# Moving the gated fusion of a GNN block from VectorE to ScalarE and GpSimd

## The chip, the cores and the metric

The kernel runs on one core of a Trainium2 chip. A core has five engines that run their own instruction streams in order[...]: PE (TensorE, matrix products and transposes), DVE (VectorE), ACT (ScalarE), POOL (GpSimd) and SP (SyncE, which only issues transfers here). POOL issues transfers as well. PEld in a profile is the weight load of TensorE. The metric is the device time of one execution in microseconds (us). The time before is the median of three runs, 2973.59 us (2967.89 to 2974.53).

## What is computed

Four graph layers run one after another on x (4096 x 256) with one 0/1 matrix adj (4096 x 4096). Each layer normalizes x, takes the positive part as h and adds its result to x. Layers 1 to 3 (a mean over neighbours, a graph attention, a dense masked attention) are not touched. The change lies in layer 0, which combines an attention branch with a gated state-space branch:

```python
Wh = h @ W
...
h_attn = attn @ Wh
h_enh = jax.nn.silu(_ln(Wh @ fe1_w + fe1_b, fe_ln_g, fe_ln_b)) @ fe2_w + fe2_b
...
hs = (h_part * jax.nn.silu(z) + h_part * D) @ out_w + out_b
c_proj = C @ cp_w + cp_b
hs = hs * (1.0 + c_proj)
comb = jnp.concatenate([h_attn, hs], axis=1)
g = jax.nn.sigmoid(jax.nn.silu(_ln(comb @ g1_w + g1_b, g_ln_g, g_ln_b)) @ g2_w + g2_b)
fused = g * h_attn + (1.0 - g) * hs + h_enh
return _ln(fused, ln_g, ln_b)
```

The kernel writes the sigmoid as (tanh(t/2) + 1)/2, and the fusion as g * (h_attn - hs) + (hs + h_enh).

## The kernel before

**Stages.** The attention of layer 0 runs to about 600 us of the profiled execution. After it comes the dense part of layer 0, to about 1200 us, then the neighbour mean of layer 1 (to about 1470 us), the attention of layer 2 and the dense attention of layer 3. Only the dense part is concerned.

**Tiling.** The 4096 rows are 32 tiles of 128 rows. The dense part takes them in NB = 8 blocks of BT = 4 tiles, so an elementwise instruction over a block of 256 features is 128 partitions x 1024 f32. `dense(b)` is a generator with 31 stretches between its yields. `run_staggered(..., 16)` starts a new block every 16 ticks, so the second half of block b is written down beside the first half of block b + 1. Blocks are called b0 to b7 here.

**What sets the order.** The stagger gives the order in which the program is written. The compiler's scheduler then settles an order for each engine, and each engine keeps it: an instruction whose input is late holds up everything behind it on the same engine.

**The steps around the change**, by line of the profile:

- L906 (DVE, x4) evacuates the gate's product from PSUM and adds the bias, into `f`, which is the block's slice of `xs` (the profile shows it as xs).
- L910 (ACT) is tanh(f/2). L911 (DVE) is (f + 1) * dh. L912 (DVE) is f * 0.5 + hs, where hs already holds hs + h_enh. dh and that sum were made by POOL at L887 and L888.
- `normed(f, "ol")`: DVE takes statistics (L123 and L124, tiles ol_st and ol_mv), L114 adds eps, POOL takes the power -1/2 (L117, ol_rs), DVE forms the offset (L750, ol_off), and ACT scales the four tiles (L753).
- L915 and L916 (POOL) multiply by the weight and add x. `measure` then takes statistics of the new x (L123 again, pl_st) for layer 1.

Beside these run steps of the next block: L857 (DVE, x4) evacuates the products of the state branch into sz, L866 (DVE, x4) those of henh, L873 (DVE, x4) those of hs. All of these matmuls (PE, L155) write into a PSUM pool `psm` of four buffers with one tag, so the fourth hs product needs the buffer that the fourth L866 frees. After hs come the transposes (L737) for the fifth matmul stage.

**A shared buffer.** `dh` of block b and `obc` of block b + 1 use one SBUF buffer:

```python
obc = d.tile([P, BT, D], F32, tag="obc", name="obc")
...
dh = d.tile([P, BT, D], F32, tag="obc", name="dh")
```

POOL writes the next obc (L815) only when the last reader of dh, L911, is done.

**Counting beside it.** The degree counts of layer 1 are taken in the same stretch. POOL issues loads of adj (L174) into four buffers, and ACT runs two Sign instructions with an accumulator on each (L181). 18 tiles of 4 quarters are counted here: 144 Sign instructions, the last of them at about 868 us. A load is issued when the Sign instructions have released its buffer.

Of the kernel before, what the change touches and what calls it, by code (L numbers as in the profile page):

```python
# [11 lines left out]
F32 = mybir.dt.float32  # L12
# [3 lines left out]
AF = mybir.ActivationFunctionType  # L16
ALU = mybir.AluOpType
# [4 lines left out]
P = 128  # L22
# [19 lines left out]
def kernel(ctx: ExitStack, tc: tile.TileContext, w: dict, out: bass.AP):  # L42
    nc = tc.nc
# [5 lines left out]
    NB = NT // BT  # L49
# [416 lines left out]
    with ExitStack() as l0:  # L466
# [10 lines left out]
        with ExitStack() as es:  # L477
# [158 lines left out]
            with ExitStack() as ps_:  # L636
                wp = ps_.enter_context(tc.tile_pool(name="l0_w0", bufs=1))
                work = ps_.enter_context(tc.tile_pool(name="l0_prep", bufs=2))
                small = ps_.enter_context(tc.tile_pool(name="l0_ps", bufs=4))
# [60 lines left out]
        with ExitStack() as es:  # L700
# [4 lines left out]
            small = es.enter_context(tc.tile_pool(name="l0_s", bufs=4))  # L705
# [68 lines left out]
            def dense(b):  # L774
# [94 lines left out]
                hs = d.tile([P, BT, D], F32, tag="hs", name="hs")  # L869
# [16 lines left out]
                dh = d.tile([P, BT, D], F32, tag="obc", name="dh")  # L886
# [15 lines left out]
                f = ha  # L902
# [5 lines left out]
                        yield  # L908

                nc.scalar.activation(f, f, AF.Tanh, scale=0.5)  # L910
                nc.vector.scalar_tensor_tensor(f, f, 1.0, dh, ALU.add, ALU.mult)  # L911
                nc.vector.scalar_tensor_tensor(f, f, 0.5, hs, ALU.mult, ALU.add)  # L912
                yield
                yield from normed(f, "ol")
                nc.gpsimd.tensor_tensor(f, f, wide(ln_g), ALU.mult)  # L915
# [3 lines left out]
                else:  # L919
                    for k in range(1, EARLY):  # L920
                        early(k)

            w1, early1 = [], []

            def early(b):

                if not w1:
                    w1.append(code_p.tile([P, KD, D], F32, tag="a", name="w1", bufs=AHEAD))
                    nc.gpsimd.dma_start(
                        out=w1[0], in_=w["L1_gnn_WT"].rearrange("(k p) m -> p k m", p=P)  # L930
                    )
                h = d.tile([P, BT, 2 * S + 1], F32, tag="bc", name="h")[:, :, 0:D]
                hT = d.tile([P, KD, BW], F32, tag="whT", name="hT", bufs=2)
                for _ in halves1(b, h, hT, w1[0], pst, psm, early1[0][:, b, :, :, :]):
                    pass

            def with_counts(b):
                n = COUNTED * NQ // NB
                for k, _ in enumerate(dense(b)):
                    if k < n:  # L940
                        tally.count(b * n + k)
                    yield
# [58 lines left out]
    with ExitStack() as es:  # L1001
# [10 lines left out]
        small = es.enter_context(tc.tile_pool(name="l1_s", bufs=4))  # L1012
# [155 lines left out]
    with ExitStack() as l3:  # L1168
# [4 lines left out]
        with ExitStack() as es:  # L1173
            wp = es.enter_context(tc.tile_pool(name="l3_w", bufs=1))
            work = es.enter_context(tc.tile_pool(name="l3_prep", bufs=2))
            small = es.enter_context(tc.tile_pool(name="l3_ps", bufs=4))
# [54 lines left out]
        small = l3.enter_context(tc.tile_pool(name="l3_small", bufs=4))  # L1231
# [165 lines left out]
```

## Time and profile before

| what | value |
|---|---|
| median of three runs | 2973.59 us |
| profiled execution, own time | 2971.09 us |
| its span | 2969.1 us |
| PE busy over the span | 2862.3 us, 96% |
| DVE, ACT, POOL busy | 1904.9, 1260.4, 960.9 us |
| L910 tanh, x8 | median 1056 ns |
| L911, x8 | 1215 to 1226 ns |
| L912, x8 | 1224 to 3007 ns, median 2478 |
| L915, POOL, x8 | 2346 to 2362 ns |
| L887, POOL, x8 | 2354 to 2382 ns |
| L815 obc, POOL, x8 | 1893 to 1912 ns |
| start of L910 in b0 to b7 | 701.92, 776.07, 850.73, 918.88, 988.08, 1057.26, 1126.43, 1179.62 us |
| 630 to 870 us: PE, DVE, ACT, POOL busy | 227.07, 116.45, 223.20, 116.57 of 240 us |
| 870 to 1150 us: the same | 275.20, 147.37, 88.35, 108.16 of 280 us |

The last two rows divide the dense part: as long as the Sign instructions run, ACT is busy for 93% of the time; after that ACT is busy for a third and PE for 98%. A busy share says which engine has little room, not which wait ends last; the chain of waits in each stretch says that.

### The profile page before, as it was taken

The page shows a single profiled execution, that of the slowest core. Times are in us where ns is not written, and L with a number is a line of the kernel's source. Part 1 is how long each engine was busy: PE and PEld are TensorE (multiplying, and loading weights), DVE is VectorE, ACT ScalarE, POOL GpSimd, SP SyncE. Part 2 cuts the span into 40 slices and gives each one's busy share as a digit, 9 for nine tenths or more (in the row PEclk, how much of TensorE's full clock was granted, in tenths as well). Part 3 has the DMA queues.
Part 4 walks back from the last instruction along what each step waited for, and adds up shares of the span by engine and source line. Part 5 has one row for each costly group of instructions (what it writes and reads, how often), then busy time and mean ns, then how long its engine had stood idle before and what let it go on. Part 6 is the DMA issues. An engine that isn't in the chain of part 4 may idle for free.

```text
span 2969.1 us, 35221 instructions
## 1 busy us (share of the span) xinstructions
PE 2862.3 (96%) x13381; PEld 2336.3 (79%) x13381; DVE 1904.9 (64%) x3491; ACT 1260.4 (42%) x1922; POOL 960.9 (32%) x725
## 2 busy tenths in 40 slices
PE   7999999999999999899999998999999999999999
PEld 6888888856556666788788777888888888888888
DVE  6877767345555554577688888656765666566553
ACT  6765555389963333994354333343111112111111
POOL 6576665545543333321055555540000000000000
PEclk9999999999999999999999999999999999999999
DMA  6966654154520001796432212002111111111100
GB/s 168 224 140 136 137 127 127 44 86 78 78 47 8 8 8 22 192 243 193 144 120 79 78 65 78 29 20 82 36 62 36 38 39 58 39 34 62 34 8 8
DMA packets 109177, 238.62 MB, mean 80 GB/s; under 512 B 10752, under 2 KB 31216, under 8 KB 100304
## 3 DMA queue, kind: packets, MB, share of 16 engines
q1 hardware_dynamic: 68512, 159.34, 15.4%
q0 software_dynamic: 37696, 69.11, 15.0%
q10 hardware_dynamic: 2800, 7.92, 0.8%
q8 instruction: 105, 1.72, 0.2%
q14 instruction: 64, 0.52, 0.1%
HBM read 265.63 MB, written 37.81 MB: 102 GB/s over the span
## 4 chain that ended last, share of the span: by engine, by line
PE 67%; DVE 8%; ACT 7%; POOL 6%; issue 6%; DMA 5%; POOLq 0%; SPq 0%; DVEq 0%; ACTq 0%
PE acc L408 16%; PE acc L1329 15%; PE s L155 15%; PE mm L155 10%; PE acc L1060 8%; POOL y L359 4%; ACT sign L181 3%; DVE run L292 3%; DVE y L355 2%; DMA turned<-codesT 2%; DMA ab_row<-l_ab_d 1%; PE q_ps L155 1%; PE tp L737 1%; DMA a<-in_adj_dram 1%; DMA l_ab_d<-abT_sb 1%
## 5 line engine op out<-in xcount | busy, mean ns | idle before, releaser
L408 PE MATMUL acc<-v,y 128*128 128x257 f32 x4096 | 929.7, 386 | 13.0 <-ACT hp L971 6.3
L408 PEld LDWEIGHTS acc<-v,y 128*128 128x128 f32 x4096 | 777.9, 192 | 126.9 <-ACT hp L971 8.0
L359 POOL TENSOR_TENSOR y<-y,turned 128x1024 f32<-128x1024 f32 (+1 forms) x272 | 549.0, 2039 | 324.8 <-DVE y L355 228.8
L387 ACT ACTIVATE y<-y,sdst 128x512 f32<-128x512 f32 (+1 forms) x544 | 350.3, 689 | 421.2 <-POOL y L359 421.1
L1329 PE MATMUL acc<-v,y 128*128 128x257 f32 x2048 | 454.5, 380 | 0.4 <-DVE rden L1337 0.4
L155 PE MATMUL s<-qT,hT 128*128 128x256 f32 x2048 | 445.2, 379 | 0.7 <-ACT qT L1277 0.7
L1322 ACT ACTIVATE y<-y 128x1024 f32<-128x1024 f32 x128 | 132.2, 1055 | 714.3 <-DVE y L1321 710.0
L155 PEld LDWEIGHTS s<-qT,hT 128*128 128x128 f32 x2048 | 389.0, 190 | 54.2 <-ACT qT L1277 1.4
L1329 PEld LDWEIGHTS acc<-v,y 128*128 128x128 f32 x2048 | 387.1, 190 | 55.9 <-issue 0.8
L355 DVE SCALAR_TENSOR_TENSOR y<-ab_row,cdst,b 128x512 f32<-128x512 f32 (+1 forms) x544 | 366.3, 709 | 64.1 <-PE acc L408 55.9
L181 ACT ACTIVATE sign<-a,limits 128x1024 bf16<-128x1024 bf16 x256 | 293.9, 1148 | 20.7 <-DMA a<-in_adj_dram 15.2
L1291 DVE SCALAR_TENSOR_TENSOR y<-code,s 128x512 f32<-128x512 bf16 x256 | 175.8, 688 | 101.0 <-PE s L155 100.7
L292 DVE SCALAR_TENSOR_TENSOR run<-turned,v,run 128x512 f32<-128x512 bf16 (+1 forms) x270 | 186.5, 691 | 59.9 <-ACT turned L536 56.4
L292 DVE SCALAR_TENSOR_TENSOR run<-turned,dst,run 128x512 f32<-128x512 bf16 x240 | 180.4, 752 | 33.7 <-DMA turned<-codesT 30.1
L1321 DVE TENSOR_TENSOR y<-y,top 128x1024 f32<-128x1024 f32 x128 | 146.2, 1213 | 43.0 <-PE top L1315 43.0
L1298 DVE TENSOR_TENSOR mx<-mx,y 128x512 f32<-128x512 f32 x224 | 154.8, 691 | 7.4
L536 ACT ACTIVATE turned<-cT,log_wide 128x1024 bf16<-128x1024 bf16 x128 | 139.1, 1104 | 41.0 <-PE cT L531 32.1
L174 POOL DMA_DIRECT2D a<-in_adj_dram x128 | 76.5, 599 | 216.1 <-ACT sign L181 161.4
L155 PE MATMUL mm<-kept 128*128 128x512 f32 x288 | 136.8, 615 | 3.3 <-ACT sz L848 2.2
L1060 PE MATMUL acc<-early,eq 128*128 128x512 f32 x512 | 129.0, 401 | 6.9 <-DVE early L457 5.3
L1060 PE MATMUL acc<-late,eq 128*128 128x512 f32 x512 | 122.8, 391 | 0.0
L1060 PEld LDWEIGHTS acc<-early,eq 128*128 128x128 f32 x512 | 96.3, 190 | 30.3 <-DVE early L457 5.5
(236 smaller groups left out, 3013.1 us busy)
## 6 DMA issues: line engine op xcount, KB each, us to landing
turned<-codesT SPq DMA_DIRECT2D x36, 1024.0 KB, 4.8
adj_t<-in_adj_dram POOLq DMA_DIRECT2D x128, 256.0 KB, 5.5
codesT<-turned SPq DMA_DIRECT2D x32, 1024.0 KB, 5.5
a<-in_adj_dram POOLq DMA_DIRECT2D x128, 256.0 KB, 4.8
code<-codesT SPq DMA_DIRECT2D x128, 256.0 KB, 5.8
code<-codesT SPq DMA_DIRECT2D x64, 512.0 KB, 7.2
ab_row<-l_ab_d ACTq DMA_DIRECT2D x14, 512.0 KB, 4.7
xt<-in_x_dram SPq DMA_DIRECT2D x8, 512.0 KB, 3.8
```

Source lines behind the costliest of these rows:

```text
L155: nc.tensor.matmul(out=ps, lhsT=lhsT_of(k), rhs=rhs_of(k), start=(k == 0), stop=(k == n - 1))
L181: nc.scalar.activation(sign, self.came[g], AF.Sign, bias=limits[:, v : v + 1], accum_out=over[:, t, v, q : q + 1],)
L292: nc.vector.scalar_tensor_tensor(to, code, dst, st["run"], ALU.subtract, ALU.min)
L355: nc.vector.scalar_tensor_tensor(y[:, :, k, :], st["ab"][:, 0, :, :], self.cdst[:, c + k : c + k + 1], st["b"], ALU.add, ALU.max,)
L359: nc.gpsimd.tensor_tensor(y, y, mask[:, :, c % QT : c % QT + 2, :], ALU.subtract)
L387: nc.scalar.activation(y[:, :, k, :], y[:, :, k, :], AF.Exp, bias=self.sdst[:, c + k : c + k + 1],)
L408: nc.tensor.matmul(out=accs[b][r], lhsT=y1[:, r, j % 2, :], rhs=self.v[:, j, 0 : D + 1], start=(j == 0), stop=(j == NT - 1),)
L1060: nc.tensor.matmul(out=acc, lhsT=eqs[c // (NT // 2)][:, ts(c % (NT // 2), P)], rhs=v1[c // BT][:, c % BT, :, :], start=(c == 0), stop=(c = ...
L1291: nc.vector.scalar_tensor_tensor(y[:, :, c : c + 2, :], st["code"][:, :, c : c + 2, :], -BIG / UNIT, ps, ALU.mult, ALU.add,)
L1298: nc.vector.tensor_tensor(mx, mx, y[:, :, c : c + 2, :], ALU.max)
L1321: nc.vector.tensor_tensor(part, part, top, ALU.subtract)
L1329: nc.tensor.matmul(out=accs[r], lhsT=st["y"][:, r, c, :], rhs=v3[:, c, :], start=(c == 0), stop=(c == NT - 1),)
```

## The change

In all blocks but the last, the two VectorE instructions become one ScalarE and two GpSimd instructions. A column of 0.5 is made once as the bias.

```diff
                 nc.scalar.activation(f, f, AF.Tanh, scale=0.5)
-                nc.vector.scalar_tensor_tensor(f, f, 1.0, dh, ALU.add, ALU.mult)
-                nc.vector.scalar_tensor_tensor(f, f, 0.5, hs, ALU.mult, ALU.add)
+                if b < NB - 1:
+
+                    nc.scalar.activation(f, f, AF.Identity, scale=0.5, bias=half)
+                    nc.gpsimd.tensor_tensor(f, f, dh, ALU.mult)
+                    nc.gpsimd.tensor_tensor(f, f, hs, ALU.add)
+                else:
+                    nc.vector.scalar_tensor_tensor(f, f, 1.0, dh, ALU.add, ALU.mult)
+                    nc.vector.scalar_tensor_tensor(f, f, 0.5, hs, ALU.mult, ALU.add)
                 yield
...
+            half = small.tile([P, 1], F32, name="half", bufs=1)
+            nc.gpsimd.memset(half, 0.5)
             w1, early1 = [], []
```

ScalarE forms 0.5 * tanh + 0.5, GpSimd multiplies by dh and adds hs. In the changed file these are L913, L914 and L915; the old L911, L912, L915 and L916 become L917, L918, L921 and L922. The dh buffer is now read last by GpSimd's own multiplication, so the next obc waits for that instead of for VectorE.

## The prediction

> **What bounds the kernel now.** I first looked at the windows of busy time, because the page's 96% for PE is a mean over stages. In the dense part there are two regimes: ACT busy 223.20 of 240 us from 630 to 870 us, PE busy 275.20 of 280 us from 870 to 1150 us. Then I asked who waits for whom on PE in the dense part (us in total, times, longest):
>
> ```profile
> PE mm L155 <- DVE henh L866: 7.9, 6, 1.9
> PE tp L737 <- ACT t L753: 6.4, 12, 2.2
> PE tp L737 <- DVE whT L741: 0.8, 1, 0.8
> ```
>
> PE loses little, and its largest loss is to the evacuation of henh, behind the changed instructions on DVE. The timeline of b4 (start, duration, engine, line; brackets: idle time before and what ended it) shows where it comes from:
>
> ```profile
> 988.08 1.06 ACT L910 ACTIVATE xs<-xs 128x1024 f32<-128x1024 f32 x1 [3.23 <-DVE xs L906]
> 989.16 1.23 DVE L911 SCALAR_TENSOR_TENSOR xs<-xs,dh 128x1024 f32<-128x1024 f32 x1 [1.12 <-ACT xs L910]
> 990.30 0.74 DVE L857 SCALAR_TENSOR_TENSOR sz<-mm,c_b_hz,sz 128x512 f32<-128x512 f32 x1
> 990.47 1.90 POOL L815 TENSOR_TENSOR obc<-kept,gain 128x1024 f32<-128x1024 f32 x1 [3.96 <-DVE xs L911]
> 990.97 2.48 DVE L912 SCALAR_TENSOR_TENSOR xs<-xs,hs 128x1024 f32<-128x1024 f32 x1
> ...
> 994.69 0.74 DVE L123 BATCH_NORM_STATS2 ol_st<-xs 128x6 f32<-128x256 f32 x2
> ...
> 997.43 1.04 POOL L117 TENSOR_TENSOR ol_rs<-ol_ve,mhalf 128x4 f32<-128x4 f32 x1 [5.07 <-DVE ol_ve L114]
> 998.50 0.16 DVE L750 SCALAR_TENSOR_TENSOR ol_off<-ol_mv,ol_rs 128x4 f32<-128x4 f32 x1 [0.83 <-POOL ol_rs L117]
> ...
> 998.70 2.08 ACT L753 ACTIVATE xs<-xs,ol_off,ol_rs 128x256 f32<-128x256 f32 x4 [9.57 <-DVE ol_off L750]
> ...
> 1000.86 2.35 POOL L915 TENSOR_TENSOR xs<-xs,kept 128x1024 f32<-128x1024 f32 x1 [2.38 <-ACT xs L753]
> 1001.19 5.34 PE L155 MATMUL mm<-kept,sz 128*128 128x256 f32 x24
> 1003.28 2.35 POOL L916 TENSOR_TENSOR xs<-xs,xt 128x1024 f32<-128x1024 f32 x1
> ...
> 1005.67 0.75 DVE L123 BATCH_NORM_STATS2 pl_st<-xs 128x6 f32<-128x256 f32 x2 [5.58 <-POOL xs L916]
> ...
> 1007.20 0.39 DVE L866 TENSOR_TENSOR henh<-mm,kept 128x256 f32<-128x256 f32 x1
> ...
> 1007.65 1.99 PE L155 MATMUL mm<-kept,sz 128*128 128x256 f32 x8 [1.11 <-DVE henh L866]
> ```
>
> DVE waits 5.58 us at pl_st for POOL, and the fourth henh evacuation stands behind pl_st. PE, otherwise without a gap, waits 1.11 us for it. So the whole chain tanh, fusion, statistics, scaling, L915, L916, pl_st, henh already ends last in every such block. It has no slack: any length added to it goes to PE. The chain of waits agrees, running through L857, ol_st, L117, L753, L915, L916 and pl_st back to PE in each of b3 to b6. In the ACT regime the same place shows as a wait of ACT:
>
> ```profile
> ACT sign L181 <- DMA a<-in_adj_dram: 4.8, 3, 2.2
> ACT xs L753 <- DVE ol_off L750: 3.7, 3, 2.1
> ```
>
> These two are most of what ACT idles there. L753 stands in ACT's order with Sign instructions behind it, and the loads for those are issued by POOL after L916.
>
> [...] L912 takes 2.48 us when L815 started 0.5 us ahead of it and 1.22 us in b7 without it. [...] here 2.35 us (L915) against 1.22 us, a ratio of 1.93. [...] Tanh without one takes 1.056 us here and Sign with a bias column 1.149 us[...].
>
> **The change part by part.**
>
> *Removed:* seven L911 and seven L912 on DVE, 7 x (1.22 + 2.48) = about 26 us of DVE time. DVE was busy for 53% of the PE regime, so this is worth only what it takes off the chain.
>
> *Added on ACT:* seven L913, a 128x1024 activation with a bias column. Nearest rows: 1.06 us (tanh) and 1.15 us (Sign). I take 1.15; both ends differ by 0.1 us. The compiled order shows no further table load. In b0 to b2 one Sign stands between tanh and L913 (1.25 us with its accumulator read); in b3 to b6 none.
>
> *Added on POOL:* L914 and L915, two SBUF inputs, 128x1024: 2.35 us each from the old L915 and L887. [...] beside the old L915 a henh took its usual 0.42 us. [...] The compiled POOL order is L914, obc (L815, 1.90), L915: the fusion's addition stands behind obc, and that is 1.9 us on the chain.
>
> *Moved on DVE:* the order becomes L906 x4, three or four L857, then ol_st, which now waits for POOL, then henh. L857 no longer stands behind L911 and L912, but PE ran through there without a gap, so an earlier L857 gains nothing. The first henh now stands behind ol_off in b3 to b6; it would be done at about 1001.4 us on b4's clock, where PE is ready at 1001.2: 0.2 us, swallowed by the larger wait later. SP's order is unchanged; PE's differs only in transposes around zT. The 0.5 column is one memset on POOL.
>
> *Chain of b3 to b6*, on the clock of b3 (tanh 918.88 to 919.94): L913 to 921.1, L914 921.2 to 923.55, obc to 925.5, L915 925.6 to 927.95 with 0.07 us between POOL instructions as in the trace. ol_st at 928.0, against 925.50 before: 2.5 us later. What follows (L117, L753, two POOL steps, pl_st, fourth henh) is as before, so PE's wait grows from 1.11 to 3.6 us. 4 x 2.5 = 10.0 us.
>
> *b0 to b2.* With the Sign between, L913 starts 2.2 us after the tanh's start. b0: tanh at 701.92, L915 ends at about 712.1, ol_st 3.6 us later than 708.53; before, an L857 (0.65 us) stood inside the statistics and now stands ahead, so ol_off is 3.05 us late. b1: ol_st at 786.3 against 782.0, less 0.55: 3.75. b2: 860.95 against 856.67, with L857 still inside: 4.3. Here ACT's order matters: L753 waits that much longer, the Sign instructions behind it too, and so do POOL's L922 and the loads behind it. Against this, between the tanh of b1 and that of b2 the compiled ACT order has 38 Sign instructions in place of 40. Two move past b2, where ACT has room: 2 x 1.27 = 2.5 us back. Sum 3.05 + 3.75 + 4.3 - 2.5 = 8.6 us. The two L174 behind the new POOL pair are issued about 5 us later in b0; with four buffers the tiles needed next have landed by then (issue to landing 4.8 us), so I charge nothing, and up to 3 us per block if that cover fails.
>
> b7 keeps its instructions, and the chain runs on through it: what b6 is late arrives whole at layer 1.
>
> **Sum.** 10.0 + 8.6 = 18.6 us on the profiled execution's own 2971.09 us (span 2969.1): 2990 us. The median shown is 2.5 us above that execution, so 2992 on that basis; I keep 2990.
>
> **Rivals.**
>
> 1. *Faster: the stall goes.* DVE freed of 3.7 us per block could reach the fourth henh before PE needs it: then the six PE waits, 7.9 us in all, vanish and the time is about 2963 us. For it: in b0 and b1 the compiled order puts all four henh ahead of pl_st, and b0's 1.9 us wait is among the six. Against it: what DVE waits for is POOL's L916, and hs (L873) is then behind pl_st instead. It decides where the new ol_st comes earlier than the old; by the rows above it comes 2.5 to 4.3 us later.
> 2. *Only ACT pays.* The longer chain is hidden somewhere and three L913 in the ACT regime remain: 3 x 1.15 = 3.5 us, 2975 us. For it: DVE and POOL have idle time. Against it: PE already waits at the chain's end.
> 3. *The Sign loads starve.* POOL's queue holds L174 behind seven us of arithmetic; three blocks lose another 3 us each[...]: about 3000 us and above.
> 4. *Nothing is changed on the chip* is out: the compiled orders differ.
>
> **How the numbers follow.** Forecast 0.74, rival 1 0.07, rival 2 with the part of the forecast that is hidden 0.09, rival 3 0.10. The forecast's own range is 2984 to 2997: 10 us from b3 to b6 are sure within 1 us, b0 to b2 give 3.5 to 12 us, and the base varies by 3 us. With rival 3's beginning and half of rival 2 the range is 2979 to 3002. A measurement here tells about 0.2%, 6 us, from no change. Faster 0.06; same 0.07; slower 0.87.
>
> **What would show it.** In the changed profile, in b3 to b6: POOL's L914, obc, L915 back to back at 2.35, 1.9 and 2.35 us; DVE idle before ol_st, released by POOL, about 3.5 us; PE's wait for the fourth henh near 3.6 us and the distance between blocks near 71.7 us instead of 69.2. In b0 to b2: ACT idle before L753 about 3.5 to 4.5 us. Wrong: ol_st no later than before, a PE wait that didn't grow, or new waits of Sign for its loads.

## The result, and the profile after

The changed kernel takes 2997.63 us (median of 4 runs, 2997.09 to 3000.11); the kernel before, run beside it on the same chip, 2973.07 us. The ratio is 1.0087, with a 95% interval of 1.0070 to 1.0105: slower by 24.6 us. The profiled execution took 2998.16 us over a span of 2996.3 us, 27.2 us more than before. DVE's busy time fell from 1904.9 to 1879.8 us, by the 25 us that were taken from it; POOL's rose from 960.9 to 992.4 us.

First the same stretch of the timeline for b4 as before (start, duration, engine, line; brackets: idle time before and what ended it):

```profile
1005.34 1.06 ACT L910 ACTIVATE xs<-xs 128x1024 f32<-128x1024 f32 x1 [3.22 <-DVE xs L906]
1006.42 1.15 ACT L913 ACTIVATE xs<-xs,half 128x1024 f32<-128x1024 f32 x1
...
1007.65 2.35 POOL L914 TENSOR_TENSOR xs<-xs,dh 128x1024 f32<-128x1024 f32 x1 [3.89 <-ACT xs L913]
...
1010.08 1.89 POOL L815 TENSOR_TENSOR obc<-kept,gain 128x1024 f32<-128x1024 f32 x1
...
1011.93 2.35 POOL L915 TENSOR_TENSOR xs<-xs,hs 128x1024 f32<-128x1024 f32 x1
1014.32 0.75 DVE L123 BATCH_NORM_STATS2 ol_st<-xs 128x6 f32<-128x256 f32 x2 [3.47 <-POOL xs L915]
...
1025.37 0.75 DVE L123 BATCH_NORM_STATS2 pl_st<-xs 128x6 f32<-128x256 f32 x2 [6.07 <-POOL xs L922]
...
1026.91 0.39 DVE L866 TENSOR_TENSOR henh<-mm,kept 128x256 f32<-128x256 f32 x1
...
1027.36 1.99 PE L155 MATMUL mm<-kept,sz 128*128 128x256 f32 x8 [3.21 <-DVE henh L866]
```

From the tanh to ol_st it is now 8.98 us, where it was 6.61 (994.69 - 988.08). DVE, with less to do, stands idle for 3.47 us ahead of ol_st and for 6.07 us ahead of pl_st, and both waits are for POOL. The fourth henh behind pl_st is late by the same amount, and PE's wait for it has grown from 1.11 to 3.21 us.

Who waits for whom on PE in the dense part, and on ACT while the Sign instructions run (us in total, times, longest), first PE:

```profile
PE mm L155 <- DVE henh L866: 17.8, 5, 4.9
PE tp L737 <- DVE whT L741: 9.8, 2, 5.0
PE tp L737 <- ACT t L753: 4.4, 4, 3.5
```

```profile
ACT xs L753 <- DVE ol_off L750: 13.0, 3, 4.8
ACT comb L738 <- PE tp L737: 6.1, 3, 5.3
ACT sign L181 <- DMA a<-in_adj_dram: 3.6, 3, 2.0
```

The waits for henh went from 7.9 us to 17.8. The 9.8 us for whT are new (0.8 before): in b0 and b1 all four henh stand ahead of pl_st, and it is the evacuation of hs (L873), behind pl_st and its statistics, that PE gets late; its copies whT are queued behind it. The ACT wait for ol_off went from 3.7 to 13.0 us. The Sign instructions wait for their loads no longer than before (4.8 to 3.6 us).

There is a second effect, which shows in the durations on PE and in its granted clock. In b2, PE's timeline of the changed kernel and then of the kernel before:

```profile
880.90 3.78 PE L155 MATMUL mm<-kept,sz 128*128 128x256 f32 x8 [4.93 <-DVE henh L866]
884.48 1.79 PE L737 MATMUL tp<-ident,v 128*128 128x128 f32 x8
886.10 1.04 PE L737 MATMUL tp<-ident,xs 128*128 128x128 f32 x8
```

```profile
869.67 1.99 PE L155 MATMUL mm<-kept,sz 128*128 128x256 f32 x8 [1.55 <-DVE henh L866]
871.50 1.04 PE L737 MATMUL tp<-ident,v 128*128 128x128 f32 x8
```

The same eight records (matmul instructions of the profile; the eight are one product group, hs3, the last of the four of hs) last 3.78 us in place of 1.99, and the transposes behind them 1.79 in place of 1.04, until PE is at full speed again some 5 us after it restarted. The granted clock in the eight records is 0.50 (880.90 to 884.68 us), in those of the kernel before 1.00 (869.67 to 871.66 us); from 886.10 us on it is 1.00 again. Below, PE resuming like this is called a slow restart. In b0 and b1 it comes behind the waits for whT:

```profile
727.93 1.97 PE L737 MATMUL tp<-ident,hs 128*128 128x128 f32 x8 [4.87 <-DVE whT L741]
...
804.50 1.97 PE L737 MATMUL tp<-ident,hs 128*128 128x128 f32 x8 [4.96 <-DVE whT L741]
```

Before, these transposes took 1.06 us in b0 and 1.25 in b1. With the products behind them, PE was longer at work by some 2 us in b0 and by 1.3 us in b1. The granted clock in both rows of transposes is 0.50. How long PE stood idle where a slow restart came is looked at in the experiments.

The windows of busy time show it too (start and end, length, busy time of PE, PEld, DVE, ACT, POOL with the number of instructions, granted clock, DMA share, GB/s), here the changed kernel from the tanh of b3 to that of b4, and from b4 to b5:

```profile
932.61:1005.34 72.73, 69.36 (x257) 44.44 (x256) 32.89 (x80) 22.48 (x32) 30.91 (x18) 0.98 0.03 8
1005.34:1076.96 71.62, 68.24 (x257) 43.32 (x256) 32.67 (x80) 22.47 (x31) 30.91 (x18) 1.00 0.03 8
```

The two blocks do the same work. The first was 1.1 us longer, all of it PE busy time, at a mean clock of 0.98. (Before, the two took 69.20 and 69.18 us.)

**Where the 24.6 us lie.** Each block is cut into two legs: from its tanh (L910) to where PE resumes after the wait (the transposes of hs in b0 and b1, the last product group of hs, hs3, from b2 on), and from there to the next tanh. All from the timelines, in us, before to after:

| block | tanh to PE resuming | longer by | PE resuming to next tanh | longer by |
|---|---|---|---|---|
| b0 | 23.18 to 26.03 | 2.85 | 50.97 to 50.50 | -0.47 |
| b1 | 22.38 to 26.07 | 3.69 | 52.28 to 53.17 | 0.89 |
| b2 | 18.94 to 23.23 | 4.29 | 49.21 to 51.71 | 2.50 |
| b3 | 19.59 to 22.02 | 2.43 | 49.61 to 50.71 | 1.10 |
| b4, b5, b6 | 19.57 to 22.02 each | 2.45, 2.45, 2.43 | 49.61 to 49.60; 49.60 to 49.61; 33.61 to 33.61 | 0 |
| sum | | 20.6 | | 4.0 |

In the second leg of b0 the slow restart does not show: PE worked some 2 us longer there, and the leg is 0.5 us shorter than before. From tanh to tanh, b0 also varies by itself: in the five kernels that leave b0 to b2 as they were (before and runs 2, 6, 7 and 9 of the experiments) it takes 74.12 to 75.57 us.

Together 24.6 us, which is also what the tanh of b7 is late (1204.21 against 1179.62). The remaining 2.6 us of the span lie behind b7, where no instruction was changed; there the profiled executions of all kernels below take between 1786.5 us and 1793.7 us, so that is within chance.

### The profile page after: what moved, and what is told of

It is laid out like the page before. It is cut to its first block, busy times and chain, and to the rows that moved or that the text cites. A ratio compares the mean times of both kernels' runs of the same rounds, so it can differ in the third digit from the quotient of the medians.

```text
span 2996.3 us, 35237 instructions
## 1 busy us (share of the span) xinstructions
PE 2874.1 (96%) x13381; PEld 2344.5 (78%) x13381; DVE 1879.8 (63%) x3477; ACT 1267.8 (42%) x1929; POOL 992.4 (33%) x740
## 4 chain that ended last, share of the span: by engine, by line
PE 57%; DVE 5%; POOL 4%; ACT 3%; DMA 3%; issue 2%; POOLq 0%; SPq 0%; DVEq 0%; ACTq 0%
PE acc L1337 15%; PE s L155 15%; PE mm L155 9%; PE acc L408 8%; PE acc L1068 8%; DMA turned<-codesT 2%; DVE y L355 2%; POOL y L359 2%; ACT sign L181 1%; DVE run L292 1%; PE tp L737 1%; PE q_ps L155 1%; POOL xs L921 1%; DMA l_ab_d<-abT_sb 1%; POOL xs L922 0%
```

## The experiments

Theory A: the chain from tanh to pl_st got longer by 2.4 to 4.3 us per block, it ends at the fourth henh or at hs, and PE pays a slow restart on top where it stood idle for long (the 3.2 us of the expectations are the wait of b3 in the changed kernel: 3.21 us, and hs3 behind it lasted 3.48; b4 to b6 have waits of 3.20 to 3.21 us too, with 1.99 behind them). Theory B: the chain alone. Theory C: ScalarE's extra work, and the order of the Sign instructions and loads. Theory D: instructions of GpSimd and DVE that last longer beside each other, as L912 did beside L815 before (2.48 us, 1.22 without it). "Intervals" are the distances between the tanh of one block and that of the next; their sum from b0 to b7 is given beside the time, since it leaves out what chance does to the other stages (before: 477.7 us).

| run | time, us | before beside it | ratio, 95% interval | intervals, sum over before |
|---|---|---|---|---|
| 1 the change in b0 to b2 | 2982.42 | 2971.85 | 1.0037 (1.0029 to 1.0045) | +13.5 |
| 2 the change in b3 to b6 | 2983.68 | 2971.85 | 1.0038 (1.0023 to 1.0053) | +16.4 |
| 3 ScalarE's part alone | 2978.39 | 2971.85 | 1.0020 (1.0009 to 1.0032) | +6.8 |
| 4 one more GpSimd step | 3020.39 | 2971.85 | 1.0160 (1.0145 to 1.0175) | +47.4 |
| 5 PE kept busy | 2995.83 | 2970.83 | 1.0077 (1.0064 to 1.0091) | +24.5 |
| 6 b3 to b6, PE kept busy | 2981.22 | 2971.37 | 1.0032 (1.0021 to 1.0043) | +10.8 |
| 7 b3 to b6, once more | 2988.89 | 2971.37 | 1.0053 (1.0041 to 1.0065) | +9.9 |
| 8 obc behind L915 | 2995.59 | 2970.83 | 1.0079 (1.0065 to 1.0093) | +25.1 |
| 9 before, obc emitted later | 2969.84 | 2970.83 | 0.9998 (0.9989 to 1.0006) | -0.1 |
| 10 before, obc later and a yield | 2973.72 | 2970.83 | 1.0010 (1.0002 to 1.0019) | +3.3 |
| 11 the change, scaling on DVE | 2979.03 | 2970.23 | 1.0023 (1.0016 to 1.0031) | +5.6 |
| 12 before, scaling on DVE | 2959.54 | 2970.23 | 0.9950 (0.9935 to 0.9965) | -10.6 |

**1 and 2. The change in some blocks only.**

```diff
-                if b < NB - 1:
+                if b < 3:
```

> The change is made in blocks b0 to b2 alone; b3 to b6 keep the two DVE instructions. Theory A (a longer chain tanh, halving, L914, obc, L915, statistics, L916, pl_st, henh or hs, plus a restart of PE at about half speed after each idle time of 3.2 us or more): tanh intervals of b0, b1, b2 grow by 2.4, 4.6 and 6.8 us as in the full change, sum 13.8 us, so about 2987. Theory B (the chain alone, no restart cost): 3.05 + 3.75 + 4.3 less 2.5 for the moved Sign, 8.6 us, about 2981.5. Theory C (ScalarE's extra work alone): 3.5 us, about 2976.5. In A the first product after the longest wait of b2 (hs3, 8 records) lasts about 3.8 us against 2.0 before.

```diff
-                if b < NB - 1:
+                if 3 <= b < NB - 1:
```

> The change is made in blocks b3 to b6 alone. Theory A: 4 x 2.45 us and, where the wait before hs3 is long enough, up to 1.5 us for one slow restart: 9.8 to 11.3 us, 2983 to 2984. Theory B: 9.8 us, 2983. Theory C: 0 to 1, since ScalarE is far from busy there, 2973 to 2974. Together with the run of the first three blocks the two should add up to the 24.6 us of the full change (A, B); if they fall short of it by more than 4 us, the two halves work on each other.

The two give 10.6 and 11.8 us, 22.4 together against 24.6: the halves add up within their intervals (2.4 and 4.5 us to either side). The first run's time does not decide: by its interval it is 8.6 to 13.4 us above before, with B's 8.6 at one end and A's 13.8 just outside the other. Its profiled execution speaks for A: the intervals of b0 to b2 grew by 2.58, 5.01 and 5.97 us, as in the full change (2.38, 4.58, 6.79), hs3 of b2 took 3.39 us behind a wait of 4.94, and the intervals behind came back to 69.17 to 69.18. For b3 to b6, theory C fails in the second run: ACT has room there, and it costs as much as the first. What had not been expected is how the second run's intervals differ among themselves: 74.09, 72.92, 71.61 and 58.22 us, 16.4 us more than before in that execution in place of 11. PE in b3 to b6 of this run:

```profile
939.19 3.78 PE L155 MATMUL mm<-kept,sz 128*128 128x256 f32 x8 [3.20 <-DVE henh L866]
...
1013.28 3.68 PE L155 MATMUL mm<-kept,sz 128*128 128x256 f32 x8 [3.20 <-DVE henh L866]
...
1086.19 1.99 PE L155 MATMUL mm<-kept,sz 128*128 128x256 f32 x8 [3.20 <-DVE henh L866]
...
1157.81 3.78 PE L155 MATMUL mm<-kept,sz 128*128 128x256 f32 x8 [3.20 <-DVE henh L866]
```

Four equal waits, three slow restarts. The block without one is 71.61 us long, those with one are 1.3 to 2.6 us longer. So a wait of 3.2 us was followed by a slow restart in some blocks and not in others.

**3. ScalarE's part alone.** L914 and L915 on DVE, as `tensor_tensor`:

```diff
-                    nc.gpsimd.tensor_tensor(f, f, dh, ALU.mult)
-                    nc.gpsimd.tensor_tensor(f, f, hs, ALU.add)
+                    nc.vector.tensor_tensor(f, f, dh, ALU.mult)
+                    nc.vector.tensor_tensor(f, f, hs, ALU.add)
```

> The halving stays on ScalarE, the multiplication and the addition are two plain two-input DVE instructions; GpSimd has nothing of the fusion. Theory A and B: the chain of b3 to b6 is longer than before only by the halving (1.15 us) and by what stands between its parts on DVE, and shorter than in the full change by two GpSimd steps of 2.35 us, obc of 1.9 and longer by two DVE steps of 1.2 to 2.5: 1.2 to 1.9 us per block over before in b3 to b6 (5 to 8 us), 1.5 to 3 in b0 to b2 (4 to 9): about 2983, no wait of PE over 3.2 us and so no slow restart. Theory C (ScalarE's part is the cause): nearly all of the loss stays, 2993 or more. Theory D[...]: it goes, 2974 or less.

6.5 us stay, so some 18 of the 24.6 us belong to GpSimd's part. The intervals of b3 to b5 are 69.42 us, only 0.24 more than before: PE's wait grew by 0.65 us (to 1.76, no slow restart), and 0.4 us of that was caught up behind it. The rest of the loss is in b1 and b2 (77.72 and 73.18 us; b0 is 2.5 us shorter than before). There PE had waits of 4.31 and 3.15 us with half speed behind them (1.85 and 1.97 us for eight transposes), where A had expected none over 3.2. A and B expected more (about 2983, 11 us above before); C's 2993 is far off, and D's 2974 lies just below the interval (2974.5 to 2981.4).

**4. One more GpSimd step in the chain.**

```diff
                     nc.gpsimd.tensor_tensor(f, f, hs, ALU.add)
+                    nc.gpsimd.tensor_scalar(f, f, 1.0, None, ALU.mult)
```

> The full change with one more GpSimd instruction in the chain behind L915 (xs times 1.0, 128x1024, one input, bound between 1.1 and 3.1 us by the rows of L810 and L851; d stands for what it lasts). Theory B: each of the seven blocks grows by d and nothing else: 7 x d, with d = 2 about 3011 and 7.7 to 21 us as bounds. Theory A: the same and, since PE's wait in b4 to b6 goes from 3.2 us to 5 us, a slow restart in each of these too, some 1.5 us each: 7 x d + 4 to 5 us, with d = 2 about 3016; hs3 (8 records) lasts over 3 us in b4, b5 and b6 where it lasts 2.0 in the full change. Theory C: under 3 us, GpSimd being off the path.

The added instruction lasts 2.795 us, so 7 x d is 19.6 us. Against the full change the time rose by 48.5 - 24.6 = 23.9 us and the intervals by 22.8, which is 7 x d and 3 to 4 us more. In b3 to b6 PE now waits 4.50 us before hs3, 1.3 us more than in the full change, and about 1.75 us for sz ahead of that, which it did not there; all four hs3 are slow (3.53, 3.78, 3.34 and 3.52 us). That is A; apart from the restarts the time grows by about what is put into the chain, as B says too.

**5. PE kept busy.** Four products ahead of hs3 that wait for the finished block and write where nobody reads:

```diff
                 for i in range(BT):
+                    if i == 3 and last:
+                        xp = last.pop()
+                        warm = pst.tile([P, BW], F32, tag="tp", name="warm")
+                        for j in range(BT):
+                            nc.tensor.matmul(
+                                out=warm[:, ts(j % 2, D)], lhsT=ident, rhs=xp[:, j, :],
+                                start=True, stop=True,
+                            )
                     ps = psm.tile([P, D], F32, tag="mm", name="mm")
...
                 if b < NB - 1:
+                    last.append(f)
                     measure(small, b, stats1)
...
+            last = []
```

> The full change with four products more per block (xs of the block just finished by the identity, 128x256, into a PSUM tile that nobody reads) ahead of hs3 in PE's order. They wait for L916, start with pl_st and last about 1.8 us, the 1.9 us that PE would go on waiting for the fourth henh. Theory A (a slow restart is paid because PE stood idle too long): the idle time is cut to about 1.3 us, hs3 lasts 2.0 us in every one of b3 to b6, and the time is 3 to 8 us below the full change, 1.3 to 2.7 us of it in each block that had a slow restart. Theory B (the chain alone; the long hs3 of single blocks has another cause): nothing is gained, 0 to 1 us more than the full change, and slow hs3 go on turning up after the wait.

In b3 to b6 it went as A says: 1.24 to 1.25 us of idle time, hs3 at full speed in all four (1.99 us), the intervals of b3 to b5 71.6 us (b3 72.73 in the full change) and that of b6 55.6 as in the full change. As a whole it did not: in b0 to b2 hs3 itself was put off until the filling products were through, PE stood idle 2.9 to 3.0 us ahead of them, and they ran at half speed in b1 (3.41 us for the eight records) and from the fifth on in b2 (2.85 us for the eight). What b2 and b3 gained, 2.2 us, was lost in b0 and b1, 2.0 us. Something else changed there too: ScalarE's order has 80 Sign instructions from the tanh of b0 to that of b2, where the full change has 77. The total cannot tell A from B.

**6 and 7. The same, where it disturbs nothing.** The change in b3 to b6 alone, with the filling products in these blocks, and its partner without them on the same chip. The first, against run 5:

```diff
-                    if i == 3 and last:
-                        xp = last.pop()
+                    if i == 3 and b > 3:
+                        xp = last[-1]
...
-                if b < NB - 1:
+                if 3 <= b < NB - 1:
```

> The change in b3 to b6 alone, with the four products that nobody reads ahead of hs3 in these blocks only; the orders of the other engines are those of the run of the last four blocks. Theory A: PE's idle time is cut from 3.2 to 1.2 us, no hs3 and no filling product is slow in any of b3 to b6, the four tanh intervals are 71.6 us each (b6 to b7 55.6), the sum over b0 to b7 is 9.8 us above before, and the time 9 to 10 us above before. Theory B': slow products after a wait come by chance and have nothing to do with the length of PE's idle time: one to three of the four blocks again show hs3 or the filling products over 3 us.

> The run of the last four blocks once more on the same chip, as the partner of the run with the filling products. Theory A: PE waits 3.2 us before hs3 in each of b3 to b6; one to four of the four hs3 last over 3 us, not necessarily in the blocks of the first time, each with an interval 1 to 2.7 us above 71.6; the sum over b0 to b7 lies 12 to 18 us above before, and the time 1 to 6 us above its partner's. Theory B': the same number of slow hs3 as in the partner, no difference in time.

PE of the filled run around b4; the other three blocks are the same to 0.01 us:

```profile
1008.61 1.99 PE L875 MATMUL warm<-xs,ident 128*128 128x256 f32 x8 [1.24 <-POOL xs L930]
1010.57 1.99 PE L155 MATMUL mm<-kept,sz 128*128 128x256 f32 x8
```

Its intervals are 71.63, 71.61, 71.62 and 55.62 us, and its time is 9.85 us above before: the chain alone, 4 x 2.45. The partner takes 2988.89 us, 7.7 us more, and the two intervals of the ratio (1.0021 to 1.0043, 1.0041 to 1.0065) only just touch. So with useless work added, the kernel is faster. But the profiled execution of the partner shows no slow restart at all: four waits of 3.20 to 3.21 us, four hs3 of 1.99 us. It was the shortest of its five executions (2983.02; the others 2986.83 to 2990.42), so the others had something more, of which no trace was kept. Their mean granted clock was lower, 0.985 to 0.987 against 0.989 in the profiled one, and lower than in any of the 13 executions of the kernel before on that chip (0.988 to 0.990) or the 8 of run 6 (0.988 to 0.992). That fits slow restarts in b3 to b6, where alone the partner differs from before; where the clock was low is not on record, so it is likely, not shown. For the profiled execution, that one to four of the four would be slow was a miss.

All profiled executions in which PE waited over 1 us ahead of hs3 in b3 to b6 (in runs 5 and 6 ahead of the filling products, in run 8 ahead of the last two groups), by the length of the wait:

| wait | kernels | slow restarts |
|---|---|---|
| 1.1 to 1.8 us | before, its copy in run 9, b3 to b6 of run 1, run 3 | 0 of 16 |
| 1.2 us | runs 5 and 6 | 0 of 8 |
| 3.2 us | after, runs 2 and 7 | 4 of 12 |
| 3.9 us | run 8 | 4 of 4 |
| 4.5 us | run 4 | 4 of 4 |

In b0 to b2, over all kernels, waits for henh, whT or the filled block of 2.4 to 3.5 us were followed by half speed in 7 of 12 cases, those of 3.9 us and more in 9 of 9, once (b1 of run 8) only from the ninth record on.

**8. obc off the chain.** Its lines were moved behind the evacuation of henh; in GpSimd's order obc then stands behind L915.

```diff
-                obc = d.tile([P, BT, D], F32, tag="obc", name="obc")
-                nc.gpsimd.tensor_tensor(
-                    obc, wide(out_b), gain.broadcast_to([P, BT, D]), ALU.mult
-                )
                 yield
...
+                obc = d.tile([P, BT, D], F32, tag="obc", name="obc")
+                nc.gpsimd.tensor_tensor(
+                    obc, wide(out_b), gain.broadcast_to([P, BT, D]), ALU.mult
+                )
                 hs = d.tile([P, BT, D], F32, tag="hs", name="hs")
```

> The full change with obc (L815, 1.9 us) behind L915 in GpSimd's order. Theory A and B: ol_st comes 1.9 us earlier in every block. In b0 to b2 that goes to the time, 1.9 us each and fewer slow restarts; in b3 to b6 the compiled order of DVE puts the third henh behind pl_st too, so that PE resumes 1.9 us earlier but with one product group of 1.8 us more to do: 0 to 0.3 us each. Sum 5 to 10 us below the full change. If only the GpSimd order counted it would be 7 x 1.9 = 13 us below. Theory C: no change against the full change.

No clear difference from the full change: 1.0079 against 1.0087 by the ratios, with intervals that overlap, and by the medians 24.8 us above the kernel before beside it, against 24.6. So the sum is a miss. The intervals show why: b0 to b2 are shorter than in the full change by 1.0, 1.5 and 4.2 us, as expected, but b3 to b6 are longer by 0.5, 2.6, 1.3 and 2.6. There PE waits before two product groups, because the third henh is behind pl_st as well; it waits longer (3.86 us) and restarts slowly in all four:

```profile
1017.77 6.42 PE L155 MATMUL mm<-kept,sz 128*128 128x256 f32 x16 [3.87 <-DVE henh L862]
```

In run 11, sixteen such records in one group took 3.83 us after a wait of 0.91. What POOL gave, the new order of DVE and the restarts took back.

**9 and 10. The kernel before with obc emitted later, without and with a yield.** The same move in the kernel before, and then a `yield` ahead of `measure`, which puts the fourth henh ahead of the last pl_st.

> The kernel before with obc emitted later, so that it doesn't run beside L912 on DVE. Theories A and B (the chain from tanh to the fourth henh ends last): L912 lasts 1.22 us in place of 2.48, ol_st comes up to 1.26 us earlier, PE's wait of 1.11 us in b3 to b6 falls to 0.2 or less, those of b0 and b2 shrink by 1.3: 5 to 7 us below the kernel before. If that chain has slack somewhere: no change against the kernel before.

> As the run before, and the fourth henh one pl_st earlier in DVE's order in b3 to b6 (two in b0 and b2). Theories A and B: what is left of PE's wait there, 0 to 0.4 us per block, goes too: 5 to 9 us below the kernel before. If the chain has slack: as the run before, no change.

The move changed nothing: POOL stands idle for 3.97 us until L911 releases obc, so obc starts at the same time as before, and L912 still lasts 2.48 us. This run is a copy of the kernel before, and shows what two equal kernels differ by: 0.02% (-0.11 to +0.06). The yield was a real miss: it made the kernel slower by 0.10% (0.02 to 0.19). PE's waits in b3 to b5 of that run:

```profile
PE mm L155 <- DVE henh L862: 2.0, 3, 0.7
PE tp L737 <- DVE whT L741: 1.8, 3, 0.6
```

The wait for henh fell from 1.1 to 0.7 us a block, and 0.6 us turned up for whT, a step further on. The chain has two ends: DVE does the fourth henh and hs both behind pl_st, and an earlier henh only hands the wait on to hs. To gain there, the chain itself must get shorter. In b3 to b6 this makes 0.1 us a block; 2.8 of the 3.3 us that the profiled execution lost lie in b0 to b2, and they are not explained.

**11 and 12. The chain shortened elsewhere.** For b0 to b6 the two GpSimd instructions behind the normalisation go to DVE, which stands idle just then; once with the full change, once with the kernel before.

```diff
-                nc.gpsimd.tensor_tensor(f, f, wide(ln_g), ALU.mult)
-                nc.gpsimd.tensor_tensor(f, f, xt, ALU.add)
+                eng = nc.vector if b < NB - 1 else nc.gpsimd
+                eng.tensor_tensor(f, f, wide(ln_g), ALU.mult)
+                eng.tensor_tensor(f, f, xt, ALU.add)
```

> The full change kept whole, and for b0 to b6 the two GpSimd instructions behind the normalisation (times ln_g, plus xt; 2.35 us each) made DVE's (1.22 us each), which DVE does while it would wait for them. The same chain, shortened at another place by 2.3 us. Theory A and B: the chain is then as long as in the kernel before, to 0.2 us; tanh intervals of b3 to b6 come back to 69.2 to 69.5 us from 71.6, those of b0 to b2 to within 1 us of before; no wait of PE over 2 us, so no slow restart: 2971 to 2977. Theory C (ScalarE's extra work, or the order of Sign) and D (GpSimd and DVE in each other's way at the fusion): what they blame is still there, 2990 or more.

> The kernel before with the same two instructions (times ln_g, plus xt) moved from GpSimd to DVE for b0 to b6. Theory A and B: the chain is 2.3 us shorter than before, which takes away both of its ends, the fourth henh (1.1 us of waiting in b3 to b6) and hs behind it (0.6 us in the run with the yield): intervals of b3 to b6 68.0 to 68.2 in place of 69.2, b0 and b2 1 to 2 us shorter, in all 6 to 9 us below the kernel before, near 2964. If DVE, with two instructions more per block, holds something else up: no change or slower.

With everything that the change does still in it, the intervals of b3 to b5 are 69.27 to 69.28 us, against 71.6 and more in the full change and 69.17 to 69.20 before; that of b6 is 53.28, against 55.62 and 53.19. For b3 to b6 this is the sharpest cut against C and D, and against every cause that lies in the fusion itself. The total is 8.8 us above before, 2979.03 us where 2971 to 2977 were expected. What the profiled execution lost, 5.6 us, is in b1 and b2 (intervals 77.47 and 70.54 us against 74.66 and 68.15), and there C is not cut off. ACT there waits 13.0 us for ol_off, exactly as in the full change, since L753 stands ahead of what was shortened. And in b1 one instruction of DVE on the chain lasts 2.31 us in place of 0.16:

```profile
795.36 2.33 POOL L781 TENSOR_TENSOR xt<-xt,kept 128x1024 f32<-128x1024 f32 x1
795.40 2.31 DVE L432 SCALAR_TENSOR_TENSOR stats<-pl_mv,stats 128x4 f32<-128x4 f32 x1 [1.58 <-POOL stats L117]
```

It started 0.04 us after the POOL instruction and ended 0.02 us after it. In the other six blocks of this run it takes 0.16 to 0.17 us. The prediction has the same kind of row in L912 beside L815. What makes these instructions longer is not shown. hs is queued behind L432, so PE waited 3.96 us for whT, and restarted slowly (1.95 us for eight transposes; 1.25 in b0 of this run). What D names is thus there, but away from the fusion, and not only here: in b0 and b1 of the kernel before, L804 on DVE (0.69 us by itself) lasts 2.78 and 2.77 us beside L888 on POOL; in the changed kernel L804 goes free there, and L801 on DVE (0.17 us by itself) lasts 1.56 and 1.81. What that is worth in b0 and b1 was not measured.

The kernel before gains 10.7 us by the same move, ratio 0.9950 (0.9935 to 0.9965); it beats both kernels. 6 to 9 us were expected. The order of DVE that came out is better than thought, with the third and fourth henh around the two moved instructions and ahead of pl_st:

```profile
992.41 1.23 DVE L916 TENSOR_TENSOR xs<-xs,kept 128x1024 f32<-128x1024 f32 x1 [1.81 <-ACT xs L753]
992.79 7.07 PE L155 MATMUL mm<-kept,sz 128*128 128x256 f32 x32
993.56 0.42 DVE L866 TENSOR_TENSOR henh<-mm,kept 128x256 f32<-128x256 f32 x1
993.89 1.22 DVE L917 TENSOR_TENSOR xs<-xs,xt 128x1024 f32<-128x1024 f32 x1
995.02 0.42 DVE L866 TENSOR_TENSOR henh<-mm,kept 128x256 f32<-128x256 f32 x1
995.36 0.74 DVE L123 BATCH_NORM_STATS2 pl_st<-xs 128x6 f32<-128x256 f32 x2
```

PE runs through all 32 records of hs without a gap; from tanh to tanh it is busy for 67.34 of 67.41 us. The intervals of b3 to b5 are 67.40 to 67.41 us, where 68.0 to 68.2 were expected. PE's idle time per interval fell from 1.20 to 0.07 us (before: 67.98 busy of 69.18), and 0.64 us went out of its busy time as well; why is left open.

## Why the prediction was right, and where its sum was off

It said slower, 2990 us with a range of 2979 to 3002; measured were 2997.63. The 18.6 us of the sum became 24.6. The direction was right, and so was the mechanism in b3 to b6, with the chain there to 0.2 us. That the total fell into the range was in part luck: the forecast's own range ended at 2997, and the room above it was left for loads of Sign that come late. They did not; slow restarts, which the prediction did not know of, took their place.

- **The bound.** That the chain from tanh to the fourth henh ends last and has no slack was right. Run 11 shows it from the other side (the chain shortened elsewhere brings b3 to b5 back to 69.3 us), run 4 by adding to it.
- **Removed.** The 26 us of DVE time (25.1 measured) brought no gain that shows: DVE's waits for POOL grew instead.
- **Added.** L913 took 1.15 us, L914 and L915 2.35 each, obc between them 1.89, as taken. That a DVE instruction lasts longer beside one of POOL was not charged, and it is not seen at the fusion (L857 beside L914 took 0.75 us; all 28 of it took 0.73 to 0.75); L801 and L804, where it is seen, were not in the sum.
- **b3 to b6, 4 x 2.5 us.** Measured 2.43 to 2.45 us each, 9.8 us for 10.0. PE's wait was forecast at 3.6 us and is 3.21, because PE reached hs3 0.35 us later; the first henh stands behind ol_off, a delay that the text had named and taken for swallowed.
- **b0 to b2, 3.05 + 3.75 + 4.3 us.** Measured from tanh to PE resuming: 2.85, 3.69 and 4.29. But the place was another in b0 and b1: hs and whT, not L753 alone. ACT's wait was the one looked for; PE's, behind hs, came with it.
- **The credit of 2.5 us** for the two Sign instructions that move past the tanh of b2 was the first step that failed. They did move (38 in place of 40), but the second legs of b0 and b1 together became 0.4 us longer, not 2.5 shorter. Why stays open. In b1, ACT was busy for 68.27 us of an interval of 79.24, before for 69.44 of 74.66, so with PE waiting 5 us for whT it may no longer have been ACT that set this block's end. But the slow restarts of PE in b0 and b1 and the longer L801 and L804 lie in the same legs, and no run separates them.
- **The slow restart** was missing altogether: 2.5 us in b2 and 1.1 us in b3 of the profiled execution, and an unknown part of the second legs of b0 and b1. The prediction took a PE wait as costing its own length. The trace before has no wait for henh over 2 us; but just behind the dense part PE waits 5.25 us, and its next four records take 2.07 us, where four such records take 1.18 a little later. The granted clock in the first four is 0.50, in the later four 1.00. That could have raised the question for a forecast wait of 3.6 us. The two lines of before:

```profile
1201.42 2.07 PE L1060 MATMUL acc<-early,eq 128*128 128x512 f32 x4 [5.25 <-DVE early L457]
...
1207.41 1.18 PE L1060 MATMUL acc<-early,eq 128*128 128x512 f32 x4
```

- From 18.6 to 24.6 us: the first legs were 0.5 us shorter than forecast (20.6 for 21.1), the second legs of b0 and b1 2.9 us longer (0.4 for -2.5), and 3.6 us of slow restarts came on top in b2 and b3.
- **Rival 3** (the loads for Sign starve) is out: those waits fell from 4.8 to 3.6 us. **Rival 1** failed at its point of decision, ol_st coming later, not earlier. **Rival 2** has a true part: ScalarE alone costs 6.5 us in run 3, through its place in the chain and in b1 and b2, half-speed stretches of PE among it, not as 3 x 1.15 us.

## What to carry to other kernels

Before moving work off a busy engine, find the chain that ends last and count the move by what it does to that chain: DVE was freed of 25 us and the kernel lost 24.6, while adding two instructions to DVE where it stood waiting won 10.7. Where a forecast makes PE wait for about 3 us or more, ask what a slow restart would add: here it was 1.1 to 2.6 us a block where nothing else hid it, in a third of the cases at 3.2 us and in all of them from 3.9 on. And look at what is queued behind the instruction that is set free: an earlier henh alone only handed the wait on to hs.

## What the hardware showed that was not expected

- Equal waits of PE of 3.20 to 3.21 us were followed by half speed in 4 of 12 cases, waits of 3.86 us and more in 8 of 8, waits up to 1.8 us in 0 of 24, all in b3 to b6. Once, in b0 of run 2, it followed a wait of 1.90 us (3.58 us for the eight records); four other executions had 1.88 to 1.92 us at the same place without it. In b0 to b2, waits of 2.4 to 3.5 us went either way (7 of 12). Half speed also set in after PE had resumed: from the fifth record in b2 of run 5 (2.85 us for the first eight, 1.99 in b0), from the ninth in b1 of run 8 (5.32 us for the sixteen records behind the transposes, 3.64 in b0).
- A DVE instruction on 128x4 elements, 0.16 us by itself, lasted 2.31 us when a GpSimd instruction on 128x1024 elements, of 2.33 us, had started 0.04 us before it: a small instruction on the chain cost nearly the whole length of a large one on the other engine. A copy of 128x4 in the changed kernel (L801, 0.17 us by itself) lasted 1.56 and 1.81 us in the same way, each time until 0.03 or 0.04 us after the end of L888.
